# Three edits to a four-layer transformer kernel on one core: identity products at the start, another order of the down products, and paired low-rank products in layer 1

## The chip, the cores and the metric

The kernel runs on one core of one Trainium2 chip. The metric is the device time of one execution in microseconds (us); smaller is better. The engines are named as in the profile: PE (TensorE matmul), PEld (its weight loads), DVE (VectorE), ACT (ScalarE), POOL (GpSimd) and SP (SyncE, which here issues nearly all DMAs).

## The reference

Four layers work on `x` with 1024 tokens (4 batches of 256) and 512 features, all in float32. Each layer normalises `x` and adds an attention and a feed-forward result of the same normalised input:

```python
xn = _layernorm(x)
x = x + _L0_attn_ref(xn, ...) + _L0_ffn_ref(xn, ...)   # 32 heads of 16; 4-bit gate, up and down weights
xn = _layernorm(x)
x = x + _L1_attn_ref(xn, ...) + _L1_ffn_ref(xn, ...)   # sigmoid attention; W, bias and a routed low-rank term
xn = _layernorm(x)
x = x + _L2_attn_ref(xn, ...) + _L2_ffn_ref(xn, ...)
xn = _layernorm(x)
x = x + _L3_attn_ref(xn, ...) + _L3_ffn_ref(xn, ...)
```

Two pieces matter here. The feed-forward of layer 0 is `(silu(x Wg) * (x Wu)) Wd`, with 1376 inner features. That of layer 1 is

```python
out = einsum('bsd,od->bso', hidden_states, W) + b
scores = x @ gate_w.T + gate_b                     # four ranks: 8, 16, 32, 64
lora_outputs = stack([x @ A[:r].T @ B[:, :r].T for r in RANKS], axis=1)
# of the four the one with the largest score is added, with weight 1
```

## The kernel before

The tokens are cut into 8 tiles of 128 (`x_sb[:, t, :]`), which stay on the chip from the first load to the last store. `xT` holds the normalised input turned, features on partitions. PSUM has 8 banks of 128 partitions by 512 float32 values; a helper, `psum_banks`, opens a pool of tiles over the 8 banks for each stage, with a number of buffers for each tag, and `ps(tag, shape, name)` takes the next buffer of a tag.

**Start.** `layer0_attention` issues the loads: the first two tiles of `x`, the first halves of `wq` and `wk`, the rope table, the other six tiles, then the second halves, `wv` and `wo`. `make_identity` builds `ident` on POOL, before everything else on that engine but a few constants. From `start_order` on the order on PE, DVE, ACT and POOL is the order of the program, written out by hand (`tc.manual_schedule`). It begins with the statistics of tiles 0 and 1 (`moments`, L125 to L129), their normalisation (`normed`, L140), their transposes on PE against `ident` (`turned`, L147) and the copies to `xT` (`evac`, L96 on ACT and L98 on DVE). A loop over half-steps then runs the attention of batch 0: the products of q and k (`features`, L278), their rotation on DVE (L289, L291), the statistics of the other tiles (`moments_of`, L232, L233), scores (L376), and so on.

**Down products.** `layer0_ffn` opens the pool `ps_f0` with one tag F of 4 buffers, each of two banks. The gate and up products (L763) go to four such buffers for each half of an inner block; ACT (L776) reads out the first two, DVE (L778) the other two, POOL adds the halves (L783), and ACT and DVE make `hT` (L798, L801). One more tile (`last`, attention output) was taken from the same tag, so the last four buffers in use are numbers 1, 2, 3 and 0. Then `ps_f1` is opened with tags F and G, four banks each, and 8 sums `po[t]`, one per tile, are built over 11 blocks `k` of `wd` (`product`, L731). For the first five blocks the loop runs over all 8 tiles; then tiles 0 to 3 are finished, and tiles 4 to 7 one after the other, between steps of the next layer's normalisation. `down_weights` (L718 to L723, DVE and POOL) makes each block's weights just before.

**Layer 1.** `layer1_weights` loads the weights; `b1` holds the 64 rows of the low-rank matrix B and, as a 65th row, the bias. `layer1` has no hand-written order: a planner orders its instructions by priority (program order) and by its own estimate of when each is ready, and may put them forward into gaps of the stage before. `norm` gives `val` (POOL, L897), `xT` and `qry` (DVE, L906). `ranks(g)`, once per half of the tokens, makes the 64 low-rank values and the four scores per token (L933), keeps those of the chosen rank on DVE (L941 to L956, `low`), turns them with one transpose per tile (L961) and copies them to `lowT` (ACT, L962), whose 65th row is set to one by POOL (L925). `scores(b, hp)` makes the attention weights (L973, L982, ACT L992, and the causal mask on POOL, L993). `outputs(b, att)` takes one bank for each of the two tiles of a batch and adds up in it four products with `w1` (L1010), one with `lowT` and `b1` over 65 partitions (L1013), and the attention products (L1018, and for the second tile L1026); DVE adds the bank to `x_sb` (L1033). `V` has two buffers.

Of the kernel before, what the change touches and what calls it, by code (L numbers as in the profile page):

```python
# [21 lines left out]
F32 = mybir.dt.float32  # L22
# [4 lines left out]
ALU = mybir.AluOpType  # L27
# [3 lines left out]
P = 128  # L31
B, T, C = 4, 256, 512
# [23 lines left out]
def block_stack(ctx: ExitStack, tc: tile.TileContext, d: dict, out: bass.AP):  # L56
# [14 lines left out]
    def ps(tag, shape, name):  # L71
        return banks["pool"].tile(shape, F32, tag=tag, name=name, bufs=banks["tags"][tag])
# [78 lines left out]
    def layer0_attention(hook, aside, xp, wd):  # L151
# [13 lines left out]
        with (  # L165
# [31 lines left out]
            for i in range(3):  # L197
# [7 lines left out]
            start_order.enter_context(  # L205
                tc.manual_schedule(engines={E.PE, E.DVE, E.Activation, E.Pool})
            )
            first_two = moments((0, 1))
            xns = [normed(t, first_two, patterns) for t in range(2)]
            for t in range(2):  # L210
# [470 lines left out]
    def layer0_ffn(gu, layer1_begun, x2, wd, hi, lo, outputs):  # L681
        E = mybir.EngineType
        with (
# [137 lines left out]
            for k in early:  # L821
                if k >= 2:
                    down_weights(k)
                    down_fetch(k + 5)
                for t in range(NT):
                    product(t, po[t], k)
            l1.values_binding()
            for k in rest:
# [87 lines left out]
    def layer1(l1, after_half):  # L916
        with tc.tile_pool(name="l1s", bufs=2) as sp, psum_banks("ps_l1s", A=2, V=2, M=2, T=2):
            w, lp, val, qry = l1.w, l1.lp, l1.val, l1.qry
            H = L1_HEADS
            for step in l1.norm(1, "T"):  # L920
                step()


            lowT = lp.tile([MAX_R + 1, B * T], F32, name="lowT")
            nc.gpsimd.memset(lowT[MAX_R : MAX_R + 1, :], 1.0)  # L925

            def ranks(g):
                n = MAX_R + 4
                pr = ps("M", [P, 4, n], f"rank_{g}")
                for i in range(4):  # L930
                    t = 4 * g + i
                    for c in range(NC):
                        nc.tensor.matmul(  # L933
                            pr[:, i, :],
                            lhsT=xT[:, c, t * P : (t + 1) * P],
                            rhs=w["rank"][:, c, :],
                            start=c == 0,
                            stop=c == NC - 1,
                        )
                sc = sp.tile([P, 4, 4], F32, tag="sc", name=f"sc_{g}")  # L940
                nc.vector.tensor_tensor(sc, pr[:, :, MAX_R:n], bc(w["gate_b"], 1, 4), ALU.add)  # L941
                pair = sp.tile([P, 4, 2], F32, tag="pair", name=f"pair_{g}")
                sc2 = sc.rearrange("p t (a b) -> p t a b", b=2)
                nc.vector.tensor_tensor(pair, sc2[:, :, :, 0], sc2[:, :, :, 1], ALU.max)
                most = sp.tile([P, 4, 2], F32, tag="most", name=f"most_{g}")
                nc.vector.tensor_tensor(most[:, :, 0], sc[:, :, 1], pair[:, :, 1], ALU.max)
                nc.vector.tensor_tensor(most[:, :, 1], sc[:, :, 2], pair[:, :, 0], ALU.max)
                keep = sp.tile([P, 3, 4], F32, tag="keep", name=f"keep_{g}")
                nc.vector.tensor_tensor(keep[:, 0, :], most[:, :, 0], sc[:, :, 0], ALU.is_gt)
                nc.vector.tensor_tensor(keep[:, 1, :], pair[:, :, 1], pair[:, :, 0], ALU.is_gt)  # L950
                nc.vector.tensor_tensor(keep[:, 2, :], sc[:, :, 3], most[:, :, 1], ALU.is_gt)
                low = sp.tile([P, 4, MAX_R], F32, tag="low", name=f"low_{g}")
                nc.scalar.copy(low[:, :, 0:8], pr[:, :, 0:8])
                for k in range(3):
                    r = slice(8 << k, 16 << k)
                    nc.vector.tensor_tensor(  # L956
                        low[:, :, r], pr[:, :, r], bc(keep[:, k, :], 2, 8 << k), ALU.mult
                    )
                tp = ps("T", [MAX_R, 4, P], f"lowT_{g}")
                for i in range(4):  # L960
                    nc.tensor.transpose(tp[:, i, :], low[:, i, :], ident)  # L961
                nc.scalar.copy(  # L962
                    lowT[0:MAX_R, g * 512 : (g + 1) * 512], tp.rearrange("p t i -> p (t i)")
                )

            def scores(b, hp):

                t0 = b * T
                s0 = ps("A", [P, 2, 2 * P], f"l1s0_{b}_{hp}")
                s1 = ps("A", [P, 2, P], f"l1s1_{b}_{hp}")  # L970
                for i in range(2):
                    h = 2 * hp + i
                    nc.tensor.matmul(  # L973
                        s0[:, i, :],
                        lhsT=xT[:, h, t0 : t0 + P],
                        rhs=qry[:, h, t0 : t0 + T],
                        start=True,
                        stop=True,
                    )
                for i in range(2):  # L980
                    h = 2 * hp + i
                    nc.tensor.matmul(  # L982
                        s1[:, i, :],
                        lhsT=xT[:, h, t0 + P : t0 + T],
                        rhs=qry[:, h, t0 + P : t0 + T],
                        start=True,
                        stop=True,
                    )
                a0 = sp.tile([P, 2, 2 * P], F32, tag="a0", name=f"a0_{b}_{hp}", bufs=4)
                a1 = sp.tile([P, 2, P], F32, tag="a1", name=f"a1_{b}_{hp}", bufs=4)  # L990
                for a, s in ((a0, s0), (a1, s1)):
                    nc.scalar.activation(a, s, AF.Sigmoid, scale=4.0 * P**-0.5)  # L992
                    nc.gpsimd.affine_select(  # L993
                        out=a[:, :, 0:P],
                        in_=a[:, :, 0:P],
                        pattern=[[0, 2], [1, P]],
                        compare_op=ALU.is_ge,
                        fill=0.0,
                        base=0,
                        channel_multiplier=-1,  # L1000
                    )
                return a0, a1

            def outputs(b, att):
                for tt in range(2):
                    t = 2 * b + tt
                    cols = slice(t * P, (t + 1) * P)
                    po = ps("V", [P, C], f"l1o_{t}")
                    for c in range(NC):
                        nc.tensor.matmul(  # L1010
                            po, lhsT=xT[:, c, cols], rhs=w["w1"][:, c, :], start=c == 0, stop=False
                        )
                    nc.tensor.matmul(po, lhsT=lowT[:, cols], rhs=w["b1"], start=False, stop=False)  # L1013
                    for h in range(H):
                        a0, a1 = att[h // 2]
                        o = po[:, h * P : (h + 1) * P]
                        f = slice(h * P, (h + 1) * P)
                        nc.tensor.matmul(  # L1018
                            o,
                            lhsT=a0[:, h % 2, tt * P : (tt + 1) * P],  # L1020
                            rhs=val[:, 2 * b, f],
                            start=False,
                            stop=h == H - 1 and tt == 0,
                        )
                        if tt == 1:
                            nc.tensor.matmul(  # L1026
                                o,
                                lhsT=a1[:, h % 2, :],
                                rhs=val[:, 2 * b + 1, f],
                                start=False,  # L1030
                                stop=h == H - 1,
                            )
                    nc.vector.tensor_tensor(x_sb[:, t, :], x_sb[:, t, :], po, ALU.add)  # L1033

            before = None
            for b in range(B):
                if b % 2 == 0:
                    ranks(b // 2)
                att = [scores(b, hp) for hp in range(H // 2)]
                if before is not None:  # L1040
                    outputs(*before)
                if b == 2:
                    after_half()
                before = b, att
            outputs(*before)


# [1032 lines left out]

    def layer1_weights(pool):
        w = {n: load(pool, n) for n in ("w1", "rank", "bqk")}
        w["b1"] = pool.tile([MAX_R + 1, C], F32, name="b1")
        nc.sync.dma_start(out=w["b1"][0:MAX_R, :], in_=d["b1_rank"])
        nc.sync.dma_start(out=w["b1"][MAX_R : MAX_R + 1, :], in_=d["b1_bias"])
        w["gate_b"] = pool.tile([P, 4], F32, name="gate_b")
        nc.gpsimd.dma_start(out=w["gate_b"], in_=bc(d["gate_b"], 0, P))
        w["bv"] = pool.tile([P, L1_HEADS, P], F32, name="bv")
# [165 lines left out]
```

## Time and profile before

| | |
|---|---|
| median of 3 runs | 1428.4 us (1426.82 to 1429.14) |
| the profiled execution | 1424.28 us, of which its span is 1422.6 us |
| mean granted clock of PE | 0.988 |
| busy share of the span | PE 96%, PEld 75%, DVE 63%, POOL 52%, ACT 36% |
| the start, until PE's first instruction | 7.7 us |
| down products L731 | 176 records, 364.2 to 441.0 us |
| layer 1, L933 to the last L1033 | 442.7 to 514.9 us |
| low-rank products L1013 | 16 records, median 593 ns each |
| transposes L961 | 8 records, median 272 ns each |

A product of float32 shows as two records, and a transpose as one. Records of PE are pipelined: their lengths overlap, so the distance from start to start is what a record costs when PE is the bound. A row of the timeline gives the start, the duration from the first start to the last end of the merged instructions, the engine, the line, the tile written and the tiles read, the shape, the count, and in brackets the idle time of the engine before it with what ended it.

### The profile page before, as it was taken

The numbers are of one execution on the slowest core, as the hardware profiler recorded it, in microseconds if no ns is written. First come the engines' busy times: TensorE is split into PE (matmuls) and PEld (weight loads), VectorE is DVE, ScalarE is ACT, GpSimd is POOL, SyncE is SP. The second block draws the span as 40 slices with busy tenths as digits, with TensorE's granted clock in tenths as the row PEclk, the third lists the DMA queues.
The fourth block names the chain that finished last, engine by engine and source line by source line (L and its number), as shares of the span: only waits on it lengthen the run. The fifth ranks groups of instructions, "written<-read, shape, count | busy, mean of one in ns | idle before, by whom it ended". The sixth has DMA issues, their size and how long they took to land.

```text
span 1422.6 us, 20817 instructions
## 1 busy us (share of the span) xinstructions
PE 1359.7 (96%) x7300; PEld 1066.8 (75%) x7300; DVE 899.1 (63%) x2370; ACT 509.8 (36%) x1333; POOL 738.0 (52%) x761
## 2 busy tenths in 40 slices
PE   7989999899999999999999999999999999989998
PEld 5656666588446677878887888888888788767887
DVE  6787777478926348635655756656557555858654
ACT  2344434387112213223232332333333333535430
POOL 3455546377733027555775956858659575210200
PEclk9999998999999999999999999999999999999999
DMA  5021223300510022011311203112222000302001
GB/s 194 2 58 35 45 45 76 86 0 3 156 61 15 1 82 75 0 45 34 105 41 60 67 16 100 60 45 64 68 63 86 30 16 16 118 1 112 0 1 60
DMA packets 50811, 76.15 MB, mean 54 GB/s; under 512 B 16475, under 2 KB 23798, under 8 KB 50322
## 3 DMA queue, kind: packets, MB, share of 16 engines
q1 hardware_dynamic: 49778, 73.77, 17.0%
q8 instruction: 58, 0.95, 0.3%
q10 hardware_dynamic: 816, 0.79, 0.2%
q0 software_dynamic: 112, 0.26, 0.1%
q14 instruction: 47, 0.39, 0.1%
HBM read 66.89 MB, written 7.91 MB: 53 GB/s over the span
## 4 chain that ended last, share of the span: by engine, by line
PE 79%; DVE 14%; ACT 2%; issue 2%; POOL 1%; DMA 1%; SPq 0%; DVEq 0%; ACTq 0%; POOLq 0%
PE m L1363 16%; PE m L1327 14%; PE dn L731 5%; PE gu L763 5%; PE s L1707 4%; PE av L1780 4%; PE m L1349 3%; PE m L1339 3%; PE half L278 3%; PE st L435 2%; PE s L1711 2%; PE l1o L1010 2%; DVE masked L389 2%; PE av L1781 2%; PE half L318 2%
## 5 line engine op out<-in xcount | busy, mean ns | idle before, releaser
L1755 POOL TENSOR_TENSOR p<-p,rs 128x512 f32<-128x512 f32 (+1 forms) x128 | 107.7, 863 | 242.3 <-DVE rs L1752 239.2
L1773 ACT COPY q<-pT 128x512 f32<-128x512 f32 x64 | 37.5, 586 | 280.1 <-PE pT L1764 280.1
L1741 ACT ACTIVATE p<-p,nm 128x256 f32<-128x256 f32 (+1 forms) x256 | 113.4, 451 | 54.4 <-DVE nm L1725 54.3
L1752 DVE RECIPROCAL rs<-sums 128x4 f32<-128x4 f32 x64 | 11.4, 178 | 178.1 <-ACT p L1741 177.8
L1327 PE MATMUL m<-xT,wq_b 128*128 128x256 f32 x448 | 105.6, 384 | 4.4 <-DVE x_sb L1577 3.0
L389 DVE CUSTOM_DVE_ANT_0 masked<-s,cmask 128x256 f32<-128x256 f32 (+1 forms) x256 | 89.8, 351 | 11.1 <-PE s L376 1.6
L1327 PEld LDWEIGHTS m<-xT,wq_b 128*128 128x128 f32 x448 | 83.1, 193 | 15.2 <-DVE x_sb L1577 3.4
L1310 POOL TENSOR_TENSOR c<-c,z 128x512 f32<-128x512 f32 x28 | 36.5, 1302 | 111.1 <-DVE c L1309 41.7
L1363 PE MATMUL m<-wo_b,o 128*128 128x256 f32 x384 | 90.2, 381 | 0.0
L449 POOL TENSOR_SCALAR_AFFINE_SELECT keys<-keys 128x256 f32<-128x256 f32 x128 | 57.0, 457 | 63.3 <-ACT keys L445 59.7
L1379 POOL TENSOR_TENSOR q<-q,t 128x512 f32<-128x512 f32 x64 | 85.3, 1334 | 6.1 <-DVE t L1378 6.1
L1378 DVE TENSOR_TENSOR t<-m,rope_sb 64x512 f32<-64x512 f32 (+1 forms) x144 | 86.3, 599 | 1.9
L1412 DVE TENSOR_TENSOR x_sb<-x_sb,m 128x512 f32<-128x512 f32 x82 | 54.5, 680 | 50.7 <-PE m L1363 40.7
L445 ACT ACTIVATE keys<-st 128x384 f32<-128x384 f32 x128 | 57.3, 488 | 75.3 <-PE st L435 75.3
L1725 DVE CUSTOM_DVE_ANT_0 p<-s,cmask 128x256 f32<-128x256 f32 (+1 forms) x256 | 76.2, 354 | 10.4 <-PE s L1707 8.0
L1363 PEld LDWEIGHTS m<-wo_b,o 128*128 128x128 f32 x384 | 70.8, 190 | 10.8 <-DVE t L1378 2.3
L1327 PE MATMUL m<-x_s,wq_t 128*128 128x256 f32 x320 | 75.5, 380 | 3.3 <-DVE x_sb L1412 2.2
L731 PE MATMUL dn<-wd,hT 128*128 128x512 f32 x176 | 76.4, 593 | 2.3 <-DVE sb L778 2.3
L783 POOL TENSOR_TENSOR sa<-sa,sb 128x1024 f32<-128x1024 f32 x22 | 62.2, 2832 | 30.3 <-DVE sb L778 30.3
L1789 ACT COPY o<-av 128x512 f32<-128x512 f32 x64 | 37.7, 589 | 89.1 <-PE av L1781 88.9
L1327 PEld LDWEIGHTS m<-x_s,wq_t 128*128 128x128 f32 x320 | 59.7, 190 | 12.7 <-DVE x_sb L1412 2.6
L1707 PE MATMUL s<-kv,q 128*128 128x256 f32 x256 | 66.4, 382 | 0.0
(329 smaller groups left out, 3483.3 us busy)
## 6 DMA issues: line engine op xcount, KB each, us to landing
wq_b<-in_wq SPq DMA_DIRECT2D x38, 256.0 KB
wo_b<-in_wo SPq DMA_DIRECT2D x32, 256.0 KB
raw<-in_wo SPq DMA_DIRECT2D x16, 512.0 KB
wkv_b<-in_wkv SPq DMA_DIRECT2D x16, 256.0 KB
wos_d<-wos_row SPq DMA_DIRECT2D x28, 128.0 KB
gate_q<-in_gate_q SPq DMA_DIRECT2D x11, 256.0 KB
up_q<-in_up_q SPq DMA_DIRECT2D x11, 256.0 KB
wq3s_b<-in_wq SPq DMA_DIRECT2D x8, 256.0 KB
```

The costliest lines, as they stand in the source:

```text
L389: nc.vector.tensor_tensor_reduce(out=ap.tile([P, T], F32, tag="masked", name="masked", bufs=1)[:, 0:n], in0=self.s[part][i][:, e, :], in1= ...
L731: nc.tensor.matmul(po, lhsT=hT[:, k, t * P : (t + 1) * P], rhs=wd[:, k, :], start=k == 0, stop=k == NBLK - 1,)
L763: nc.tensor.matmul(p[:, half], lhsT=w[:, g, :], rhs=x[half][:, g], start=k == 0, stop=k == 1,)
L783: nc.gpsimd.tensor_tensor(self.a, self.a, self.b, ALU.add)
L1327: nc.tensor.matmul(out[:, i, :], lhsT=b[:, c, i * P : (i + 1) * P], rhs=a[:, c, :], start=start and i == 0 and c == 0, stop=i == 1 and c == 1,
L1363: nc.tensor.matmul(out[:, t, :], lhsT=a[:, c, t * P : (t + 1) * P], rhs=b[:, c, :], start=start and t == 0 and c == 0, stop=t == 1 and c = ...
L1378: nc.vector.tensor_tensor(t2[at], src[of], sin[of], ALU.mult)
L1379: after(1, lambda: nc.gpsimd.tensor_tensor(dst, dst, t2, ALU.add))
L1707: nc.tensor.matmul(s1[:, i, :], lhsT=q[:, i, P:T], rhs=kt[:, 0, :], start=True, stop=True)
L1725: nc.vector.tensor_tensor_reduce(out=x[f"p{part}"][:, e, :], in0=x[f"s{part}"][:, e, :], in1=cmask if part else cmask[:, P : 2 * P], scale ...
L1741: nc.scalar.activation(p, p, AF.Exp, bias=x["nm"][:, part, e : e + 1], scale=-1.0, accum_out=x["sums"][:, part, e : e + 1],)
L1755: nc.gpsimd.tensor_tensor(p, p, bc(x["rs"][:, part, :], 2, n), ALU.mult)
```

## The change

Three edits, independent of each other.

First, 18 products of `ident` with itself are put at the head of PE's order, into a tile of their own that nothing reads:

```diff
+            idle = ps("A", [P, P], "idle")
+            for _ in range(18):
+                nc.tensor.matmul(idle, lhsT=ident, rhs=ident, start=True, stop=True)
             first_two = moments((0, 1))
```

Second, in the first five blocks of the down products the tiles come in the order 2 to 7, 0, 1:

```diff
                     down_fetch(k + 5)
-                for t in range(NT):
+                for t in (*range(2, NT), 0, 1):
                     product(t, po[t], k)
```

Third, in layer 1 the low-rank values of two tiles are turned together, those of the first tile of a batch to partitions 0 to 63 and those of the second to 64 to 127; `b1` holds B twice, once in each half; the low-rank products of a batch's two tiles follow each other, each with 64 rows; and the bias is loaded as a row for all partitions and added to `x_sb` by POOL, tile by tile:

```diff
-            lowT = lp.tile([MAX_R + 1, B * T], F32, name="lowT")
-            nc.gpsimd.memset(lowT[MAX_R : MAX_R + 1, :], 1.0)
+            lowT = lp.tile([P, NT // 2, P], F32, name="lowT")
+            for t in range(NT):
+                nc.gpsimd.tensor_tensor(x_sb[:, t, :], x_sb[:, t, :], w["bias"], ALU.add)
...
-                tp = ps("T", [MAX_R, 4, P], f"lowT_{g}")
-                for i in range(4):
-                    nc.tensor.transpose(tp[:, i, :], low[:, i, :], ident)
-                nc.scalar.copy(
-                    lowT[0:MAX_R, g * 512 : (g + 1) * 512], tp.rearrange("p t i -> p (t i)")
-                )
+                tp = ps("T", [P, 2, P], f"lowT_{g}")
+                for i in range(2):
+                    nc.tensor.transpose(
+                        tp[:, i, :], low[:, 2 * i : 2 * i + 2, :].rearrange("p t r -> p (t r)"), ident
+                    )
+                nc.scalar.copy(lowT[:, 2 * g : 2 * g + 2, :], tp)
...
             def outputs(b, att):
-                for tt in range(2):
-                    t = 2 * b + tt
-                    cols = slice(t * P, (t + 1) * P)
-                    po = ps("V", [P, C], f"l1o_{t}")
+                pos = [ps("V", [P, C], f"l1o_{2 * b + tt}") for tt in range(2)]
+                cols = [slice((2 * b + tt) * P, (2 * b + tt + 1) * P) for tt in range(2)]
+                for po, at in zip(pos, cols):
                     for c in range(NC):
                         nc.tensor.matmul(
-                            po, lhsT=xT[:, c, cols], rhs=w["w1"][:, c, :], start=c == 0, stop=False
+                            po, lhsT=xT[:, c, at], rhs=w["w1"][:, c, :], start=c == 0, stop=False
                         )
-                    nc.tensor.matmul(po, lhsT=lowT[:, cols], rhs=w["b1"], start=False, stop=False)
+                for tt, po in enumerate(pos):
+                    r = slice(MAX_R * tt, MAX_R * tt + MAX_R)
+                    nc.tensor.matmul(
+                        po, lhsT=lowT[r, b, :], rhs=w["b1"][r, :], start=False, stop=False
+                    )
+                for tt, po in enumerate(pos):
+                    t = 2 * b + tt
                     for h in range(H):
...
-        w["b1"] = pool.tile([MAX_R + 1, C], F32, name="b1")
-        nc.sync.dma_start(out=w["b1"][0:MAX_R, :], in_=d["b1_rank"])
-        nc.sync.dma_start(out=w["b1"][MAX_R : MAX_R + 1, :], in_=d["b1_bias"])
+        w["b1"] = pool.tile([P, C], F32, name="b1")
+        for half in (slice(0, MAX_R), slice(MAX_R, P)):
+            nc.sync.dma_start(out=w["b1"][half, :], in_=d["b1_rank"])
+        w["bias"] = pool.tile([P, C], F32, name="b1_row")
+        nc.sync.dma_start(out=w["bias"], in_=bc(d["b1_bias"], 0, P))
```

## The prediction

> **What bounds the kernel now.** I read the page first (engines, slices), then the chain of waits by order of time, then the timeline at the three places that the change touches, and the rows of PE alone around them.
>
> ```profile
> PE 1359.7 (96%) x7300; PEld 1066.8 (75%) x7300; DVE 899.1 (63%) x2370; ACT 509.8 (36%) x1333; POOL 738.0 (52%) x761
> ```
>
> PE is the bound over the whole. So each place is asked: does PE idle or run slowly there, and what ends last? An fp32 product is two records; I call "pitch" the distance from one record's start to the next.
>
> The start, from the timeline (start, duration, engine, line, and in brackets the idle time before and what ended it):
>
> ```profile
> 1.23 0.29 POOL masks.py:199 TENSOR_SCALAR_AFFINE_SELECT ident<-ident 128x128 f32<-128x128 f32 x1
> ...
> 7.73 1.94 PE L147 MATMUL lnT<-ident,xn 128*128 128x128 f32 x8 [7.73 <-DVE xn L140]
> ...
> 10.35 3.78 PE L278 MATMUL half<-xT,wq_sb 128*128 128x256 f32 x8 [0.68 <-ACT xT L96]
> ...
> 11.01 0.69 DVE L232 BATCH_NORM_STATS2 st<-x_sb 128x6 f32<-128x512 f32 x1 [1.46 <-DMA x_sb<-in_x]
> ...
> 13.92 2.66 PE L278 MATMUL half<-xT,wk_sb 128*128 128x256 f32 x8
> 14.16 0.42 DVE L289 TENSOR_TENSOR qs<-half,rope_sb 128x256 f32<-128x256 f32 x1 [1.45 <-PE half L278]
> ...
> 16.42 1.89 PE L278 MATMUL half<-xT,wq_sb 128*128 128x256 f32 x8
> 16.62 0.42 DVE L289 TENSOR_TENSOR qs<-half,rope_sb 128x256 f32<-128x256 f32 x1 [0.54 <-PE half L278]
> ```
>
> The same eight records take 3.78, 2.66 and 1.89: PE runs at half speed and then at full speed. (The view by stretches gives a granted clock of 1.00 here, but its first event comes later; the pitches, 0.43 against 0.216, decide.) Solving 2.50 = 0.427a + 0.216(8-a) for the second group puts the step at 15.5, 5.1 us after unbroken work began at 10.35. From 16.62 to 31 DVE is dense and PE waits for it.
>
> The changes of PSUM pool, rows of PE:
>
> ```profile
> 270.12 0.50 PE L763 MATMUL gu<-x_hi,gate_w 128*128 128x512 f32 x1 [0.54 <-DVE tr L481]
> ...
> 364.23 4.13 PE L731 MATMUL dn<-wd,hT 128*128 128x512 f32 x9 [2.31 <-DVE sb L778]
> ...
> 442.68 3.79 PE L933 MATMUL rank<-rank_sb,xT 128*128 128x68 f32 x32 [0.68 <-ACT o L727]
> ```
>
> Each time PE starts just when the **last** reader of the old pool ends (269.62 + 0.45; 362.90 + 1.28; 442.04 + 0.59).
>
> Layer 1, timeline:
>
> ```profile
> 447.13 1.20 DVE L946 TENSOR_TENSOR most<-sc,pair 128x4 f32<-128x4 f32 x1
> ...
> 449.54 1.53 POOL L897 TENSOR_TENSOR val<-xn,v_hard 128x512 f32<-128x512 f32 x1 [1.23 <-DVE xn L140]
> ...
> 452.64 0.60 PE L961 MATMUL lowT<-ident,low 128*64 128x128 f32 x4 [1.08 <-DVE low L956]
> ...
> 458.71 1.02 PE L1013 MATMUL l1o<-b,lowT 65*128 65x512 f32 x2
> ```
>
> From 460 to 510 PE is busy all of the time, so what PE saves there ends the layer earlier. The order in this layer is the planner's, not written by hand.
>
> **Part 1, identity products.** Added: 18 products, 36 records, behind `ident` (ready at 1.52). Half speed: 36 x 0.213 (the transposes' pitch at 7.73) = 7.7 us, until 9.3; full speed: 36 x 0.11 (transposes at 447, 8 in 1.04) = 4.0. If the step comes 5.1 us after 1.6 as it did after 10.35: 24 records slow until 6.7, 12 fast, end at 8.0. Then the transposes end at 8.9 (not 9.7), ACT's copy (0.59) at 9.6, and the first product stands at 9.65 to 11.5 instead of 10.35 to 14.13. What is late next is DVE: it waits for the third input tile until 11.01, and with two statistics is free at 12.7. So its two waits go, 1.45 + 0.54 = 2.0, and not the 2.6 that PE gains. If the train stays slow until 9.3, products from 10.9 end at 12.8: still 1.9. All that follows to 31 us is DVE's dense queue, and it moves with it; the weights' second halves, issued by 12, are first read after 24, and transfers are quiet by then (share 0.09 from 20 to 30 us). I take **-2.0**; bounds: -2.0, and +1.7 if the train does not lift the speed (rival B).
>
> The Trainium skill (TensorE: Matmul & The Clock Gate, Parts 1 and 4) has PE at half rate until a free-running window of some 3.4 us was busy, and does not count transposes as busy; by that alone, an estimate, the step comes between 5.1 and 8.5 us, and the sum is the same, for DVE hides the difference. On transposes the trace does not decide: eight of them, not unbroken with what followed, lifted nothing.
>
> **Part 2, order of the down products.** Moved: tiles 0 and 1 behind 2 to 7, for the first five rows of `wd`. Bank by bank, the last evacuation (DVE `sb`, to 364.18) frees banks 0 and 1 only; banks 2 to 7 are read out at 360.3, 361.7 and 363.0, so PE could go on at 361.76 and win 2.3 (six tiles x 0.86 cover the rest). But 442.68 speaks against it: of the eight banks of the down products seven had been read by 436.6, and `rank` still waited for the eighth; and at 270.12 the first block sum waited for the last reader of a bank of the other tag. The wait seems to belong to the pool, not to the bank. Then any first tile waits for 364.18. I take **0**, since all three rows are alike; bounds 0 and -2.3. Nothing else moves: weights and sums of five rows come in the same order.
>
> **Part 3, layer 1.** PE removed: 8 transposes become 4, 4 x 0.11 = 0.45. Eight low-rank products (0.86 each, two records x 0.43) become four pairs in two row groups. The nearest rows:
>
> ```profile
> 19.96 1.14 PE L376 MATMUL s<-kT,qT 32*128 32x512 f32 x8
> ...
> 492.93 1.06 PE L1149 MATMUL flat_b<-xT,ar_sb 128*32 128x512 f32 x8
> 493.92 1.12 PE L1013 MATMUL l1o<-b,lowT 65*128 65x512 f32 x2
> 494.88 0.97 PE L1163 MATMUL route<-gather,flat 128*128 128x24 f32 x8
> ...
> 533.03 1.12 PE L1874 MATMUL core_out<-bw_sb,cores_sb 16*128 16x512 f32 x2
> 534.09 1.99 PE L1327 MATMUL m<-x_s,wq_t 128*128 128x256 f32 x8
> ```
>
> Four row groups of 512 columns, eight records, last 1.14 where one after the other would last 3.44: groups do run together. But a change of grouping costs: `core_out` holds PE 1.06 (to 534.09) where two plain records hold 0.86, and the plain product behind `flat_b` 0.96 (to 494.88). With 0.1 on either side a pair is 1.15 against 1.72: 4 x 0.57 = 2.3. Bounds: 4 x 0.86 = 3.4 saved; or, if groups of 64 rows (none in the trace) do not overlap, 4 x 0.3 = 1.2 lost. I take 2.3, nearest to the row-grouped ones. Together with the transposes PE saves **2.75**.
>
> The Trainium skill (TensorEngine Tiling (Array Packing), Key Properties) says that a change of tiling mode drains the array, which speaks against this edit, and the rows above agree with some 0.1 on either side. Its "up to 2x" (Theoretical Speedup) taken alone, an estimate, would save 3.4.
>
> POOL: eight additions of 128x512 at 1.27 (such rows of POOL stand at 394 to 406 us) replace one memset of 1.23. POOL is idle at 428.4 to 432.5 and 435.2 to 445.6; tiles 0 to 3 are readable for it by then, and the memset shows that POOL's work of this layer is put forward into such gaps (370.09). Tiles 4 to 7 are not readable before 446 and 450, when POOL is at work (5.83 of 10 us). There they hold up DVE: a 128x4 operation took 1.20 and 1.25 beside POOL's `val`, against 0.16 at 470. Two or three more such stops of 1.05 delay `low`, at which PE stands already for 1.08: 0 to 2.5 given back. I take **1.2**, half, as further products (the second bank's, 3.44 us) can be drawn ahead. The masks queued behind the additions on POOL, four selects of 0.42 for the first batch, slip from 454.7 to at most 459; PE needs them 3.4 later than before, at about 462: nothing. If POOL were busy throughout, rival C. DVE's final additions wait for the bias, which is there before 460.
>
> Waits for a second bank per batch: the sum that frees it ends 0.9 after the batch before, the first bank's products last 3.44: nothing; without them 0.9. SP: one more issue and a wider one, 0.4 to 0.7 each, in SP's gap from 366.2 to 371.2; 0.38 MB at 293 GB/s is 1.3 us, first read at 458: nothing, and with no gap the next issues, for rows needed 27 us later, slip by 1.
>
> Net **-1.5** (bounds -3.9 and +3.3: 1.2 lost, 0.45 saved, 2.5 given back).
>
> **Sum.** -2.0 + 0 - 1.5 = -3.5. The profiled execution took 1424.28 (span 1422.6 and 1.7 around it), so 1420.8 for its like; the runs' median is 1428.4, 4.1 above it, and I set the sum against that: **1424.9**. A difference of 0.2%, 2.9 us, is about what a measurement of this kernel can tell from no change.
>
> **Rivals.** A: banks are waited for one by one; -5.8, 1422.6. For it: the numbering of the banks; against: 442.68. Chance 0.13. B: the identity products do not lift the speed; the train ends at 9.3, slow transposes at 11.0, copy 11.9, the slow first product at 15.9 against 14.13: +1.7 - 1.5, 1428.6. For it: the transposes at 7.73 lifted nothing. 0.12. C, slower: all eight additions come after 446, ahead of `val` and the masks. DVE's chain to `low` loses 8 x 1.05 = 8.4, PE stands at `lowT`; less 2.75 and 2.0 that is +3.6, 1432.0. It ends slower than before once `low` slips by more than 4.75 us. Against: the idle POOL at 428 to 445. 0.10. D: the row groups do not overlap: -2.0 + 1.2 - 0.45 + 1.2 = 0, 1428.4. 0.07. The forecast keeps 0.58; its own range is -1 to -5.
>
> **How the numbers follow.** 1421.0 to 1429.0 holds forecast, A, B and D and leaves out C and the best sums. Faster by over 0.2%: 0.58 x 0.72 + A 0.13 = 0.55. Slower: C, 0.08, and tails 0.02. The rest, 0.35, is within. The granted clock, 0.89 between 30 and 60 us, shows that PE is also slowed for a few us there; where such a stretch falls may shift, which is in the tails.
>
> **What would show it.** The first product of L278 starts near 9.65 with eight records in 1.9, and the waits 1.45 and 0.54 of DVE L289 are gone, that on DMA staying; the first `dn` still waits for DVE `sb`, for about 2.3; the pairs' four records of L1013's successor within 1.2; `low` a little later, PE's wait before `lowT` 1 to 3.5. I am wrong if `dn` starts with no wait, if the products at 10 us are slow, or if PE stands long before `lowT` or the masks.

## The result and the profile after

The changed kernel took 1427.1 us (median of 14 executions, 1418.1 to 1430.3) against 1428.5 for the kernel before (14 executions, 1420.3 to 1431.5). The ratio is 0.9989, with a 95% interval from 0.9973 to 1.0005. That cannot be told from no change; of the forecast -3.5, some -1.4 was left. The profiled execution even took 1428.38 (span 1426.7) against 1424.28 before. Why single executions mislead here is the last part of the story.

The first line of the page after: PE's busy share is as before, and POOL is busy for 9 us more.

```profile
PE 1368.7 (96%) x7332; PEld 1072.6 (75%) x7332; DVE 903.3 (63%) x2370; ACT 509.6 (36%) x1333; POOL 747.0 (52%) x768
```

**The start**, from the timeline of the changed kernel (start, duration, engine, line):

```profile
1.57 6.37 PE L211 MATMUL idle<-ident 128*128 128x128 f32 x36 [1.57 <-POOL ident masks.py:199]
...
7.78 1.14 PE L147 MATMUL lnT<-ident,xn 128*128 128x128 f32 x8
...
9.60 1.99 PE L282 MATMUL half<-xT,wq_sb 128*128 128x256 f32 x8 [0.68 <-ACT xT L96]
10.04 0.69 DVE L236 BATCH_NORM_STATS2 st<-x_sb 128x6 f32<-128x512 f32 x1 [0.93 <-DMA x_sb<-in_x]
...
11.43 1.89 PE L282 MATMUL half<-xT,wk_sb 128*128 128x256 f32 x8
...
11.66 0.41 DVE L293 TENSOR_TENSOR qs<-half,rope_sb 128x256 f32<-128x256 f32 x1
...
13.48 0.39 DVE L293 TENSOR_TENSOR qs<-half,rope_sb 128x256 f32<-128x256 f32 x1
```

The train ends at 7.94 (forecast 8.0), the first product stands at 9.60 (9.65) with its eight records in 1.9, and both waits of DVE on PE are gone (rows without brackets). The first rotation stands at 11.66 instead of 14.16, the second at 13.48 instead of 16.62.

**The down products**, PE's timeline: the wait is there as before, 2.32 for 2.31.

```profile
364.97 15.29 PE L735 MATMUL dn<-wd,hT 128*128 128x512 f32 x35 [2.32 <-DVE sb L782]
```

**Layer 1**, three timelines, of PE, DVE and POOL:

```profile
450.71 0.63 PE L147 MATMUL lnT<-ident,xn 128*128 128x128 f32 x4 [0.40 <-DVE xn L140]
452.12 0.63 PE L147 MATMUL lnT<-ident,xn 128*128 128x128 f32 x4 [0.78 <-DVE xn L140]
...
455.53 0.41 PE L968 MATMUL lowT<-ident,low 128*128 128x128 f32 x2 [1.92 <-DVE low L963]
...
461.38 5.32 PE L1016 MATMUL l1o<-w_sb,xT 128*128 128x512 f32 x12
...
466.63 1.13 PE L1021 MATMUL l1o<-b,lowT 64*128 64x512 f32 x4
467.69 1.38 PE L1030 MATMUL l1o<-val,a 128*128 128x128 f32 x10
```

```profile
449.66 2.31 DVE L140 TENSOR_SCALAR xn<-x_sb,mv,rstd 128x512 f32<-128x512 f32 x2
451.89 1.23 DVE L956 TENSOR_TENSOR keep<-most,sc 128x4 f32<-128x4 f32 x1
...
453.12 1.24 DVE L958 TENSOR_TENSOR keep<-sc,most 128x4 f32<-128x4 f32 x1
```

```profile
437.83 1.72 POOL L932 TENSOR_TENSOR x_sb<-x_sb,b_row 128x512 f32<-128x512 f32 x1
446.31 1.50 POOL L902 TENSOR_TENSOR val<-xn,v_hard 128x512 f32<-128x512 f32 x1 [6.76 <-DVE xn L140]
447.78 1.27 POOL L932 TENSOR_TENSOR x_sb<-x_sb,b_row 128x512 f32<-128x512 f32 x1
...
453.06 1.28 POOL L932 TENSOR_TENSOR x_sb<-x_sb,b_row 128x512 f32<-128x512 f32 x1
```

The kernel before had, on DVE and on PE:

```profile
448.93 0.99 DVE L140 TENSOR_SCALAR xn<-x_sb,mv,rstd 128x512 f32<-128x512 f32 x2
...
451.09 0.38 DVE L951 TENSOR_TENSOR keep<-sc,most 128x4 f32<-128x4 f32 x1
```

```profile
460.47 3.60 PE L1010 MATMUL l1o<-w_sb,xT 128*128 128x512 f32 x8
463.90 1.02 PE L1013 MATMUL l1o<-b,lowT 65*128 65x512 f32 x2
464.76 0.39 PE L1018 MATMUL l1o<-val,a 128*128 128x128 f32 x2
```

The pair works: its four records hold PE for 1.06 (466.63 to 467.69) where two products held 1.72 (0.86 each, 463.90 to 464.76). But the 12 records ahead of it take 5.25 to its start, and at the pitch before (eight in 3.43) they would take 5.15. The additions of tiles 0 to 3 end by 439.6, in POOL's old gap. Those of tiles 4 to 7 alternate with `val` from 446.3 to 457, and DVE stops beside them: two `xn` take 2.31 (0.99 before), and one more 128x4 operation takes 1.24 (0.38 for its like before). It ends at 454.36, and the addition beside it at 454.34. PE's waits ahead of `lowT` add up to 0.40 + 0.78 + 1.92 = 3.1, before 1.08. The view by stretches adds what no step of the forecast had (columns: stretch, its length, busy time of PE, PEld, DVE, ACT, POOL, the granted clock, the DMA share, GB/s):

```profile
450.00:456.50 6.50, 3.40 (x21) 2.47 (x21) 6.50 (x11) 2.61 (x8) 6.50 (x6) 1.00 0.00 1
456.50:459.90 3.40, 3.40 (x10) 2.38 (x9) 1.85 (x3) 1.29 (x3) 3.19 (x7) 0.51 0.00 0
459.90:465.00 5.10, 5.10 (x18) 2.91 (x17) 0.00 (x0) 0.87 (x2) 0.77 (x2) 0.99 0.00 0
```

PE was busy for half of 6.5 us, and then ran for 3.4 us at a clock of 0.51.

Cut at three landmarks of PE's timeline, layer 1 is the same to 0.01 us in every profile of one version:

| us | first `rank` to `lowT` | `lowT` to second `rank` | second `rank` to layer 2's first product | sum |
|---|---|---|---|---|
| before (and identity products alone) | 9.96 | 13.91 | 48.46 | 72.33 |
| changed (and third edit alone) | 12.11 | 14.94 | 46.91 | 73.96 |
| third edit without POOL's additions | 9.96 | 13.25 | 46.86 | 70.07 |
| third edit, four additions later | 9.96 | 13.26 | 46.92 | 70.14 |
| third edit, PE's wait filled | 13.70 | 13.23 | 46.91 | 73.84 |

(The expectations below count the stage to another product of layer 2, 1.0 us later: 73.3 for 72.33, 74.9 for 73.96.)

### The profile page after: what moved, and what is told of

Its sections match the earlier page's. It is cut to its first block, busy times and chain, and to the rows that moved or that the text cites. A ratio compares the mean times of both kernels' runs of the same rounds, so it can differ in the third digit from the quotient of the medians.

```text
span 1426.7 us, 20887 instructions
## 1 busy us (share of the span) xinstructions
PE 1368.7 (96%) x7332; PEld 1072.6 (75%) x7332; DVE 903.3 (63%) x2370; ACT 509.6 (36%) x1333; POOL 747.0 (52%) x768
## 4 chain that ended last, share of the span: by engine, by line
PE 79%; DVE 14%; ACT 3%; issue 2%; POOL 1%; DMA 1%; SPq 0%; DVEq 0%; ACTq 0%; POOLq 0%
PE m L1375 16%; PE m L1339 14%; PE dn L735 5%; PE gu L767 5%; PE s L1719 4%; PE av L1792 4%; PE m L1361 3%; PE m L1351 3%; PE half L282 3%; PE st L439 2%; PE l1o L1016 2%; PE s L1723 2%; DVE masked L393 2%; PE av L1793 2%; PE half L322 2%
## 5 line engine op out<-in xcount | busy, mean ns | idle before, releaser
L1375 PEld LDWEIGHTS m<-wo_b,o 128*128 128x128 f32 x384 | 70.8, 190 | 10.8 <-DVE t L1390 2.3
```

Source lines behind the costliest of these rows:

```text
L1375: nc.tensor.matmul(out[:, t, :], lhsT=a[:, c, t * P : (t + 1) * P], rhs=b[:, c, :], start=start and t == 0 and c == 0, stop=t == 1 and c = ...
```

## The experiments

The theory: each part does at its place what its rows say, and stretches at half the clock, of 3.4 us or a multiple, decide the rest. They lie elsewhere in each profile, and where the change makes PE sparse it brings one of its own.

### The parts alone

`train_only` is before with the first diff alone.

> Before plus the 18 identity products. Theory 1 (the gain is real at its place, and stretches at the half clock, which fall elsewhere, take it back): the first q product stands at 9.6 with eight records in 1.9 to 2.0, DVE's first rotation starts near 11.7 without the wait of 1.45, and the tr<-half operations of the first 50 us are 3.1 us earlier than before. The first gate product then comes 3 us earlier (near 267) if as many half-clock stretches lie before it as before the change, and 1.6 us later than that for each further stretch of 3.4 us; between runs that have the same stretches the time is 3 us lower (median near 1425.5, 1424 to 1428). Rival (the start's gain is lost in a queue behind it, whatever the clock does): at 50 us nothing or little of the 3.1 is left, and the median is 1428.4. Second rival (work that starts earlier brings a half-clock stretch with it at 70 us each time): the stretch of 13.7 us at 71 is there, as in the changed kernel, and the first gate product is at 270.

Median 1425.4, ratio 0.9989 (0.9972 to 1.0007); the start is as in the changed kernel. The first gate product of this profile stands at 274.2, later than before's 270.1: from 20 to 265 us its stretches at half clock sum to 47.8 us, before's to 23.9. Since single profiles are that far apart, I compared the start over all 14 profiles of this study. DVE's fourth rotation stands at 19.51 to 20.75 without the train (8 profiles, mean 20.10) and at 16.94 to 17.91 with it (6 profiles, mean 17.38): the gain is **2.7**. The second rival falls too: a stretch of 13.7 us begins at 75.4 and 75.5 in the profiles of `order_only` and `layer1_only`, which have no identity products.

`order_only` is before with the second alone.

> Before with the other order of the down products alone. Theory (a PSUM pool's first tile waits for the last reader of the pool before it): the first dn still waits 2.3 us for DVE sb, the stage from the first gate product to the first rank product is as before within 0.2 us, and the time is 1428.4 within 2. Rival (bank by bank): the wait is gone or under 0.5, the stage is 2.3 us shorter, 1426.1.

The wait is there (2.32), the stage is 94.1 + 78.4 as before, the median 1429.4. The ratio, 1.0020 (1.0004 to 1.0036), comes with a mean granted clock of 0.9820 over its executions against 0.9838 of before's, and no stage shows it.

`order_tile` is `order_only` with another setting for one pool:

```diff
-        with tc.tile_pool(name=name, bufs=1, space=PSUM) as pool:
+        waits = "tile" if name in ('ps_f1',) else "pool"
+        with tc.tile_pool(name=name, bufs=1, space=PSUM, reuse_waits=waits) as pool:
```

> Before with the other order, and with the pool ps_f1 of the down products told to wait tile by tile for the banks' former readers. Theory (the wait belongs to the pool): now the first dn follows the last gate or up product with a wait under 0.5 us, tile 0's first product comes after 364, and the stage from the first gate product to the first rank product is 2.0 to 2.3 us shorter: 1426.2 where the clock's stretches are as before. Rival 1 (the banks themselves are the bound, since tile 2's bank is read out late): the wait stays over 1.5 us. Rival 2 (PE gains the 2.3 and waits later for hT or the weights of the next blocks, since DVE makes them): the first wait is gone, and a new wait of 1 to 2.3 us stands before the second or third block; the stage is as before.

PE's timeline of this kernel, around the change of pool:

```profile
363.77 0.40 PE L763 MATMUL gu<-x_lo,up_w 128*128 128x512 f32 x1
364.00 21.19 PE L731 MATMUL dn<-wd,hT 128*128 128x512 f32 x49
```

No wait is left, and the gate and up products' stage lasts 91.6 instead of 94.1, with nothing lost behind it (78.4 from there to the first `rank`, as before). So the wait belonged to the pool as a whole, by its setting and not by the chip, and the order alone could not gain. Whether the setting gains as much with the old order was not run. Median 1426.0, ratio 0.9985 (0.9965 to 1.0005).

`layer1_only` is before with the third diff alone.

> Before with the third edit alone: low-rank pairs in two row groups, half as many transposes, the bias added by POOL. Theory (POOL's eight additions alternate with val between 446 and 457, they hold up DVE's chain to low and leave PE sparse, and the clock drops there): PE's waits from the first rank product to lowT sum to about 3 us (before 1.1), a half-clock stretch of 3.4 us begins near 456, the pairs take 1.1 each, and the stage from the first rank product to the first query product of layer 2 is 73.3 + 2.0 + 1.6 - 2.7 = 74.2, within 73.5 to 75. Time 1429. Rival (the layer gained 1.5 to 2.7 us by itself and the rise in the changed kernel came from its earlier start or from the other two edits): stage of 70.6 to 71.8, 1426.3.

Row two of the table: 72.33 becomes 73.96, +1.6, with the stretch at half clock at 461.3, the same 13 us behind the first `rank` as in the changed kernel. Median 1431.9, ratio 1.0024 (1.0004 to 1.0045). The third edit, meant by the forecast for -1.5, loses 1.6.

### POOL's additions

`layer1_nobias` is `layer1_only` without the additions, so the bias is missing from its result:

```diff
-            for t in range(NT):
-                nc.gpsimd.tensor_tensor(x_sb[:, t, :], x_sb[:, t, :], w["bias"], ALU.add)
```

> The third edit alone, without POOL's eight additions: the bias of layer 1's feed-forward is left out of the result. Theory (the additions of tiles 4 to 7 hold up DVE's chain to low, leave PE sparse from 455 to 461 and so bring the half-clock stretch that follows): DVE's keep and xn operations are short again, PE's waits before lowT sum to about 1.1 us as before the change, no half-clock stretch stands between 440 and 520, and the stage from the first rank product to the first query product of layer 2 is 73.3 - 0.45 (transposes) - 2.7 (four pairs at 1.06 in place of 1.72) = 70.2, within 69.8 to 70.8, against 74.9 with the additions. Rival (the pairs or the transposes themselves, which wait for both tiles of a batch and for a second bank, make PE sparse): the stage stays between 73 and 75 with the stretch in it.

`layer1_late` is `layer1_only` with the additions of tiles 4 to 7 behind the masks of the second batch:

```diff
-            for t in range(NT):
-                nc.gpsimd.tensor_tensor(x_sb[:, t, :], x_sb[:, t, :], w["bias"], ALU.add)
+            def add_bias_row(tiles):
+                for t in tiles:
+                    nc.gpsimd.tensor_tensor(x_sb[:, t, :], x_sb[:, t, :], w["bias"], ALU.add)
+
+            add_bias_row(range(4))
...
+                if b == 1:
+                    with tc.issue_after(last_mask[0].ins):
+                        add_bias_row(range(4, NT))
```

> The third edit alone, with the additions of tiles 4 to 7 moved on POOL behind the masks of the second batch. Theory: as without the additions, since those of tiles 0 to 3 lie in gaps before 446 where PE does not wait for DVE: stage of 70.2 to 71.0, no half-clock stretch, and between runs at the same mean clock 2.5 us under the kernel before (near 1426). Rival (the additions only move: the later masks, or DVE's final additions, which share a port with them or wait for them, now hold PE): a wait of 1 to 3 us before the attention products or a bank, and a stage of 72 to 74.

Rows three and four of the table: without the additions, or with four of them later, the way to `lowT` lasts 9.96 again and no stretch at half clock lies in the layer. The timelines of DVE, PE and POOL of `layer1_late`:

```profile
453.29 0.99 DVE L140 TENSOR_SCALAR xn<-x_sb,mv,rstd 128x512 f32<-128x512 f32 x2
```

```profile
457.00 0.41 PE L969 MATMUL lowT<-ident,low 128*128 128x128 f32 x2 [1.08 <-DVE low L964]
```

```profile
462.33 4.93 POOL L930 TENSOR_TENSOR x_sb<-x_sb,b_row 128x512 f32<-128x512 f32 x4
```

The four late additions lie in POOL's idle time and hold up nobody. The layer gains 2.2, not the 3.1 of my expectation, since PE pays on both sides of a pair. The last record of `w1` ahead of it takes 0.52 to the next start instead of 0.43, 0.4 in four batches. The attention products behind it last 2.78 in the new order, where those of two tiles lasted 0.89 + 1.78, another 0.4. So a pair saves 0.46 with its two sides, and not 0.66. The transposes save 0.40 and not 0.45, and PE's wait before layer 2 is 0.07 longer; with these the missing 0.9 is found. Medians 1424.5, ratio 0.9978 (0.9961 to 0.9994), and 1428.0, ratio 0.9990 (0.9967 to 1.0012).

`layer1_fill` is `layer1_only` with eight products ahead of the first turns of `low`:

```diff
+                if g == 0:
+                    for _ in range(8):
+                        nc.tensor.matmul(tp[:, 0, :], lhsT=ident, rhs=ident, start=True, stop=True)
                 for i in range(2):
                     nc.tensor.transpose(
```

> The third edit alone as it was changed (POOL's additions in their first place), with eight identity products into the bank of lowT ahead of the first turn of low; the turns overwrite them, and the result is the same. They take 16 records of 0.108, 1.7 us, and stand in PE's wait of 1.92 before lowT. Theory (a stretch at half clock follows when PE's array had too little work in the 3.4 us before it; counting each product as its columns' time times the share of rows and of columns of the array in use, the 3.4 us ahead of nearly all stretches so far held under 1.34 us of such work): the stretch after 457 is gone although POOL and DVE do the same as before, and the stage from the first rank product to the first query product of layer 2 is 74.9 - 1.6 = 73.3 (72.9 to 73.7); mean clock about 0.001 above layer1_only's, time about 1.0 to 1.6 lower. Rival (the additions' stop of DVE costs PE the whole 1.6 by itself, or the stretch has another cause, such as POOL's own activity): the stretch stays, stage 74.9 or a little more.

Half of it came. PE's timeline, DVE's, and the stretches:

```profile
453.72 2.05 PE L966 MATMUL lowT<-ident 128*128 128x128 f32 x16 [1.63 <-DVE xT L98]
455.61 0.38 PE L968 MATMUL lowT<-ident,low 128*128 128x128 f32 x2
```

```profile
448.14 2.32 DVE L140 TENSOR_SCALAR xn<-x_sb,mv,rstd 128x512 f32<-128x512 f32 x2
```

```profile
454.00:457.00 3.00, 3.00 (x26) 2.92 (x26) 2.83 (x4) 0.76 (x2) 3.00 (x5) 1.00 0.00 0
457.00:461.00 4.00, 4.00 (x19) 2.72 (x18) 0.00 (x0) 1.74 (x4) 1.99 (x6) 1.00 0.00 0
```

DVE and POOL do as in `layer1_only`, and the clock stays at 1.00: `lowT` to the second `rank` lasts 13.23, as without the additions, so the stretch at half clock had cost 14.94 - 13.25 = 1.7. But the products did not start in PE's wait as I had laid them: they take their bank from the same tag as the turned inputs and waited for DVE's copy to `xT` (1.63 in brackets). They began where `low` was nearly ready and put `lowT` off by 1.6 (13.70 for 12.11), so the stage is 73.84 and the time 1432.2, ratio 1.0025 (1.0002 to 1.0049). What the additions cost is now two terms: 2.15 for DVE's stops and 1.7 for the clock.

### What lifts PE's speed at the start

`train_turns` is `train_only` with transposes in the train:

```diff
-            for _ in range(18):
-                nc.tensor.matmul(idle, lhsT=ident, rhs=ident, start=True, stop=True)
+            for _ in range(36):
+                nc.tensor.transpose(idle, ident, ident)
```

> Before with 36 transposes of the identity in place of the 18 identity products (the same number of records). Question: does such work lift PE's speed at the start? Theory 1 (any unbroken work of PE does): as with the products, the step comes about 4.4 us after PE's start, the train ends near 8 and the first q product at 9.6 lasts 1.9 to 2.0 for eight records. Theory 2 (transposes do not count): the train runs at 0.21 us a record throughout and ends at 9.3, the transposes of the inputs last 1.9 behind it, and the first q product's eight records last over 3 us.

PE's timeline:

```profile
1.57 5.76 PE L210 MATMUL idle<-ident 128*128 128x128 f32 x36 [1.57 <-POOL ident masks.py:199]
7.58 1.32 PE L147 MATMUL lnT<-ident,xn 128*128 128x128 f32 x8 [0.25 <-DVE xn L140]
9.58 1.99 PE L281 MATMUL half<-xT,wq_sb 128*128 128x256 f32 x8 [0.68 <-ACT xT L96]
```

Transposes lift it as well as products. The Trainium skill (TensorE: Matmul & The Clock Gate, Part 4) says that transposes do not count as busy work in the same way. Here 36 records take 5.76 us, where at the slow pitch of 0.213 they would take 7.7, and the products behind them run at full speed; the measurement decides, for float32 and in the one execution that was made (1427.3 us).

### The gains together, and the clock

`best` is the changed kernel with the pool's setting of `order_tile` and the later additions of `layer1_late`.

> All three edits, with the pool of the down products waiting tile by tile and the additions of tiles 4 to 7 behind the masks of the second batch. If the gains add up: start -3.1, down products -2.3, layer 1 -2.5 to -3.1, together -7.9 to -8.5 where the clock's stretches are alike; by the mean clock's cost in the runs so far (0.87 us for each 0.001) 1420 at a mean clock of 0.982, median 1418 to 1422. Rival (an edit's gain is lost again wherever a later stage waits for something else, as DMA-fed weights): -4 to -5, 1424.

Median 1421.4, ratio **0.9947** (0.9931 to 0.9963): they add up. The gains at their places are 2.7 + 2.5 + 2.2 = 7.4, and the medians lie 7.3 apart. A straight line through all executions (an offset for each kernel, one slope) gives 0.9 us for each 0.001 of the mean granted clock, and leaves 1.1 us of scatter. At the same clock the identity products alone stand 2.7 below before, `order_only` 0.3 above, `order_tile` 2.1 below, `layer1_only` 0.6 above, `layer1_late` 1.9 below, the changed kernel 2.2 below and `best` 7.7 below, each within 0.8. The slope differs between kernels (0.5 to 1.3 in those with ten executions or more), so this is a reading and no law.

What decides the stretches? The changed kernel, by stretches, and PE's timeline just ahead of the second:

```profile
67.40:70.80 3.40, 2.22 (x13) 1.17 (x14) 3.08 (x15) 2.39 (x6) 2.02 (x5) 1.00 0.06 13
70.80:84.50 13.70, 13.66 (x78) 8.40 (x76) 8.09 (x36) 3.68 (x9) 6.21 (x11) 0.50 0.41 87
```

```profile
68.83 1.14 PE L380 MATMUL s<-kT,qT 32*128 32x512 f32 x8
69.79 1.63 PE L439 MATMUL st<-q_e,k_e 32*128 32x256 f32 x4
```

From 70.8 PE is busy for 13.66 of 13.70 us and still has half the clock. The Trainium skill (TensorE: Matmul & The Clock Gate, Part 1) has half rate as the state after an idle window of 3.4 us. The 3.4 us before this fall were not idle: PE was busy for 2.22 of them, with products on 32 rows. So I counted array work from the trace's records: columns x 0.43/512 us, times the share of rows and columns of the array in use. The profile's clock changes only on a grid of 3.413 us that begins elsewhere in every execution. Between 20 and 1400 us the 14 profiles hold 5462 such intervals at full clock. Of these 123 were followed by half clock, and 111 of the 123 held under 1.34 us of array work; of the 5339 others 31 did. The limit was chosen on these same profiles, and the 12 exceptions all lie at one place of the kernel, near 1250 us. PE's busy time, the obvious rival, sorts them worse: 56 of the 123 had PE busy for more than 2.2 us, while 60 intervals with less than 2.0 were followed by full clock. In layer 1 the interval ahead of the fall held 1.29 in the changed kernel and in `layer1_only`; with the eight products of `layer1_fill` one there held 1.40, and no fall came. Then I added work where an interval is below the limit.

`best_fill` is `best` with 14 products (its expectation counts 15), here those ahead of the turned maxima; the seven others go the same way into `st[0]` of blocks 1, 3 and 15 and into `av` of blocks 0, 2, 14 and 15. `before_fill` is before with the same 14.

```diff
+                def fill(self, out, count):
+                    for _ in range(count.get(self.n, 0)):
+                        nc.tensor.matmul(out, lhsT=ident, rhs=xT[:, 0, 0:T], start=True, stop=True)
...
                     self.maxT = hb()
+                    self.fill(self.maxT, {1: 2, 3: 2, 5: 1, 14: 1, 15: 1})
```

`best_fill32` makes each of them narrow:

```diff
-                        nc.tensor.matmul(out, lhsT=ident, rhs=xT[:, 0, 0:T], start=True, stop=True)
+                        nc.tensor.matmul(
+                            out[0:32], lhsT=ident[0:32, 0:32], rhs=xT[0:32, 0, 0:T], start=True, stop=True
+                        )
```

> The version with the three gains, and in layer 0's attention 15 products of 128x128 by 256 columns whose output is overwritten by the next instruction of PE (the result is the same), at places where the profiles have under 1.34 us of array work in 3.4: blocks 0 to 3, 5, 14 and 15. They cost 15 x 0.43 = 6.5 us of PE, of which some 3 lie in PE's waits for DVE's maxima (1.41, 0.84, 0.32 and smaller ones). Theory (array work in fixed stretches of 3.4 us decides the clock): between 39 and 262 the stretches at half clock shrink from 27 to 37 us in most profiles to 10 or less, the mean clock rises by 0.006 to 0.008 to 0.988 to 0.990, and the time falls by 0.87 us for each 0.001 less 3 us of products, so by 2 to 4: median 1417.5 to 1419.5. Rival (the clock follows something else, as time or power): the stretches stay, and the time rises by 3 to 6 to 1424 to 1427.

> As best_fill, but each of its 14 products (counted as 15 in the expectation of best_fill) uses 32 rows and 32 columns of the array only, at the same 256 columns: as long on PE, a sixteenth of the array work. Theory 1 (array work decides the clock): the stretches at half clock between 39 and 262 us are as in the version without products, 27 to 37 us, mean clock 0.982 to 0.984, and the time is that version's 1421.4 plus 0 to 3, 1421 to 1424.5. Theory 2 (PE being busy is enough): as best_fill, mean clock 0.990, 1414 to 1417.

> Before with the 14 products of best_fill alone. Theory (the stretches at half clock in layer 0 cost the kernel before some 9 us, for want of array work): mean clock from 0.984 to 0.989 to 0.991, the products cost 1.2 (as between the versions with and without them at the same clock), and the time falls by 0.87 x 6 - 1.2 = 4, to 1423 to 1425.5, with less scatter between executions. Rival (they helped only beside the three edits, whose earlier start moved the work against the stretches): time 1428 or more.

`best_fill`: 1415.2 (5 executions, 1414.2 to 1416.5), ratio **0.9918** (0.9890 to 0.9946), the lowest median of all, though the interval overlaps with that of `best`, which was measured on another chip. Layer 0's attention in the view by stretches, of `best` and then of `best_fill`:

```profile
20.00:265.00 245.00, 225.43 (x1722) 149.34 (x1720) 185.69 (x802) 101.44 (x250) 128.26 (x217) 0.93 0.20 45
```

```profile
20.00:265.00 245.00, 227.93 (x1796) 150.86 (x1794) 188.06 (x807) 102.51 (x252) 130.09 (x223) 0.96 0.20 46
```

Its stretches at half clock there shrink from 34.1 to 20.5 us, less than expected (10 or less). That is one profile each, and those of the versions without such products hold 23.9 to 47.8. The mean clock over the executions says more: it rises from 0.982 (0.980 to 0.985) to 0.990 (0.989 to 0.992). By the straight line `best_fill` stands 6.2 below before at the same clock, 1.5 less than `best`: that is what the products cost, and what they gain comes with the clock. The two others do not make it a proof. `best_fill32`, with a sixteenth of the array work, keeps 34.1 us of stretches in its profile, as theory 1 has it; but over 11 executions its mean clock is 0.987 and its median 1418.6, ratio 0.9942 (0.9921 to 0.9963), between the two theories. `before_fill` rises to 0.987 only: median 1424.5 for 1427.8, ratio 0.9993 (0.9969 to 1.0017), which tells nothing apart; its profile holds 30.7 us of stretches where before's held 23.9, and its executions scatter as widely as before's. That array work below about 1.34 us in 3.4 goes before most falls is shown by the intervals, and that more work keeps the clock up by one profile of `layer1_fill`. How much products at other places gain, and why narrow ones helped too, stays open.

## Why the prediction was right or wrong

**The total** fell into the range and into "no change that can be told" (0.35 of the chances, where 0.55 lay on faster). The sum of the terms as measured is -2.7 + 0 + 1.6 = -1.1, beside the medians' -1.4. That the total came right is in part luck: part 3 was worse than forecast by 3.1 and part 1 better by 0.7, and the range was wide enough to hold no change at all.

**Part 1** was right in its mechanism: the step of speed 4.4 us after PE's first record (forecast 5.1), the train's end at 7.9, DVE next. Its size was 2.7 for 2.0, past the bound of 2.0 that I gave. The term that was mis-sized is the bound by DVE, which I took from one profile's third input tile, 11.01. Over the 14 profiles that tile is read at 9.78 to 11.30, train or none, and the slow rotation without the train comes at 14.02 to 14.32. A bound that rests on one DMA's landing should have had a margin of 0.7 on either side.

**Part 2** was right: 0, by the rows of the three changes of pool, with the wait at 2.32. That the wait belongs to the pool was shown by `order_tile`. Rival A fell in the change and would have been right under another setting: 2.5 where I had 2.3.

**Part 3** failed, in two terms. PE's saving was 2.2 for 2.75: a pair saved 0.46 for 0.57. I had 1.15 for a pair with its sides, and it is 1.06 in itself with 0.1 ahead of it and 0.1 behind, in the attention products, which I had not looked at. POOL's price was 2.15 + 1.7 = 3.9 for 1.2. The step that failed is "Two or three more such stops of 1.05 delay `low`", of which I took "half, as further products (the second bank's, 3.44 us) can be drawn ahead": PE drew nothing ahead, its order in the layer stayed, and two more stops (1.32 in `xn`, 0.86 in `keep`) came through in full. And the sparse 6.5 us that this made brought 3.4 us at half clock, which the forecast left to "the tails" as if it fell by chance. The Trainium skill (SBUF — State Buffer) describes the port that DVE and GpSimd share as an exclusive lock, held for a whole instruction; the rows agree, for a 128x4 operation of 0.38 takes 1.24, about one addition of 1.27. Rival C's mechanism, `low` late by POOL's additions, was thus at work at a quarter of its size: 2.15 of 8.4, since tiles 0 to 3 did lie in the idle time named against it. Rivals B (the train lifted nothing) and D (no overlap of the row groups) are out.

**The clock** was under-weighted as a whole. Executions of the kernel before lie up to 12 us apart, with mean clocks from 0.979 to 0.991, so the difference of two profiles (+4.1) said nothing of the change; the landmarks of the stages did.

## What to carry to other kernels

Before work is given to an engine that is "idle", see who shares a port with it in those microseconds and what waits for that one; the same four additions cost 3.8 us beside a chain of small DVE operations and nothing that shows 7 to 11 us later. Where PE's products are narrow or sparse, look at the granted clock by stretches: a gap costs itself and perhaps a stretch at half clock behind it, and a few products into a bank about to be overwritten may cost less than that. Here they seem to have paid in `best_fill`, and did not in `layer1_fill` and `before_fill`. Compare versions by landmarks of stages and by executions at the same clock, not by two profiles.

## What was not expected of the hardware

- The clock fell to half after 3.4 us in which PE was busy for 2.22, on products of 32 rows, and stayed there with PE busy for 13.66 of 13.70; 111 of 123 falls came after 3.413 us with under 1.34 us of array work, and one stretch of 3.4 us cost 1.7 where PE was the bound.
- 36 transposes lifted PE's speed at the start as 36 records of products did (one execution).
- Two products of 64 rows in two row groups hold PE for 1.06 where two full ones hold 1.72, and cost 0.1 more on each side.
